# Two edits to the order of work in a two-layer image kernel: layer 1's spread of statistics and first-chunk normalisation one slice later, and the last image's loads and normalisation further ahead

## The chip, the core and the metric

The kernel runs on one NeuronCore of a Trainium2 chip. The metric is device time in microseconds: the kernel before takes 5440.93 us, the median of three runs from 5439.19 to 5442.27. The profile is of one execution with a span of 5433.7 us. The engines are named as the profile names them: PE is TensorE (matmuls), PEld its weight loads, DVE is VectorE, ACT is ScalarE, POOL is GpSimd, and SP is SyncE, which only issues DMA transfers. Each engine runs its own instructions in the order in which the built program has them, and waits on semaphores for the others.

## What is computed

The input is 16 images of 56 x 56 pixels with 384 channels, in float32. Two layers with residuals are applied. Group normalisation `_gn` takes mean and variance of an image over all pixels and 12 channels at a time (32 groups).

```python
# layer 0: dilated 3x3 attention in three groups of 128 channels (dilations 1, 2, 3), 4 heads each
x = x + proj(attention(qkv(_gn(x))))
# layer 1: depthwise 3x3 convolution with weights of sign -1, 0 or +1
x = x + depthwise(_gn(x), sign(clip(w)))
```

Each normalisation needs the statistics of a whole image before its first pixel can be normalised. So there are two barriers an image: `stats0` before layer 0, `stats1` before layer 1.

## The kernel before

An image is cut into 7 chunks of 8 rows (448 pixels), 112 chunks in all. For each chunk m three plans lay out work in slices, nine slices a chunk (`STEP = 9`):

- `plan_a` (stage A, slice 9(m - 9)): loads pixels, turns them to channels by pixels on TensorE, gathers `stats0`, stores to a DRAM scratch `xd`.
- `plan_b` (slice 9m): normalises, projects to k and v (`k_or_v`, tile `pkv`, copied out by ScalarE at L473) and q (`pq`), multiplies q and k on VectorE (`t`, L516), sums them on TensorE (`ps`), takes the softmax (`pt_s` at L536 is its first matmul, once a chunk), spreads the weights over channels (`pb_a`, L582), weighs v (`w`, L589 on VectorE and L597 on GpSimd, `y`), projects out (`po`, L615), adds the residual and gathers `stats1`, and stores to `x1d`. The edges of k and v are passed between neighbouring chunks by small DMA copies on SyncE's queue (the halos, L477 and L478).
- `plan_c` (slice 9(m + 10)): layer 1. It loads x1d in two ways. Channels 0 to 255 come as tiles `z` (in the last image `z_last`), with the rows above and below stacked on partitions, are normalised by ScalarE (and one set in four by VectorE in the last image) and convolved on TensorE (`pc`, L727, two a chunk). The last 128 channels come as `xg`, are normalised into `zg` by ScalarE (L756), multiplied tap by tap (`m`, L778) and summed on GpSimd; in the last image VectorE does the taps (L769). The result is turned back on TensorE (`pt_o`, L799), copied by ScalarE (`osb`, L801) and stored (L804): on SyncE's queue up to image 14, on ScalarE's in the last one.

The plans only call `at(when, order, piece)`: a piece is put in a list under its slice and a rank within the slice. At the end the pieces are run in sorted order, which gives the program order; the framework below then schedules instructions, engine by engine, close to that order. So a change of a slice number adds no instruction and moves instructions on several engines' queues.

The statistics of an image are a chain of six small pieces (`group_norm`), put down by `plan_b` of an image's last chunk at slices t0 + 27 + `STAT1_SLICE[k]`: aggregate by channel, mean (`pm`), deviation (`pb`), variance (`pv`), inversion on GpSimd (L345 to L349, tile `pair`), and the spreading `spread_out` on TensorE (`pp` at L354, `pz` at L367), whose results VectorE copies to `mr` and `mrz` (L358, L372). Layer 1's normalisation needs these two. In the kernel before, `spread_out` of layer 1 stands in slice t0 + 33, and the first chunk's `normalise_g` two slices later.

In the last image nothing else is left to run from the statistics on, and it takes other buffers, those of layer 0 that have become free. `z_last` takes pool `t_p` (4 buffers) for even chunks and `w_p` (3) with `xr_p` (1) for odd ones, two buffers for each of a chunk's two halves; so loads of chunk c + 2 wait for the convolutions of chunk c. For chunks 1 to 5 a half is loaded with four transfers (L702), each one with an access pattern of three shifted rows over 32 channels:

```python
three_rows = bass.AP(one.tensor, one.offset, [(W, 3), *one.ap])
nc.sync.dma_start(set_of(j, q), three_rows)
```

PSUM has three buffers (`ps_mt`) for most matmul results, `pkv`, `po`, `pt_x`, `pt_o`, `pc` and the statistics among them.

Of the kernel before, what the change touches and what calls it, by code (L numbers as in the profile page):

```python
# [35 lines left out]
def dilated_attention_then_binary_conv(  # L36
# [243 lines left out]
    def rows(ap):  # L280
        return ap.rearrange("p (r w) -> p r w", w=W)
# [6 lines left out]
    def in_one_go(matmuls):  # L288

        matmuls[0]()  # L290
        with tc.high_priority():
            for m in matmuls[1:]:
                tc.keep_in_program_order(m())
# [88 lines left out]
    def at(when, order, piece):  # L382

        pieces.setdefault((when, order), []).append(piece)
# [60 lines left out]
    def plan_b(m, t0):  # L445
# [181 lines left out]
        def norm(k):  # L627
            if k == 0:
                steps["of"] = group_norm(stats1.pop(b), lambda mr, mrz: mr1.update({b: (mr, mrz)}), True)
            steps["of"][k]()  # L630
# [20 lines left out]
        if c == NCH - 1:  # L651
            for k in range(6):
                at(t0 + 27 + STAT1_SLICE[k], STAT_ORDER[k], lambda k=k: norm(k))

    def plan_c(m, t0):

        b, c = divmod(m, NCH)
# [3 lines left out]
        def edges(j):  # L661
            found = []
            for z, _, _ in had[f"z{j}"]:
                if c == 0:
                    found.append(z[0:HD, :, 0:W])
                if c == NCH - 1:
                    found.append(z[2 * HD : 3 * HD, :, PX - W : PX])
            return found

        def set_of(j, q):  # L670
            return next(z[:, q - q0] for z, q0, q1 in had[f"z{j}"] if q0 <= q < q1)

        def load(j):
            by_set = x1d[b].rearrange("(j q c) n -> j c q n", q=NQ, c=HD)[j]
            if b < B - 1:
                z = z_p.tile([P, NQ * PX], F32, tag="z", name="z")[:K3].rearrange("p (q n) -> p q n", q=NQ)
                had[f"z{j}"] = [(z, 0, NQ)]
            else:

                had[f"z{j}"] = []  # L680
                for q0 in range(0, NQ, 2):
                    pool, tag = (t_p, "t") if c % 2 == 0 else (w_p, "w") if (j, q0) != (1, 2) else (xr_p, "xr")
                    z = pool.tile([P, 3, PX], F32, tag=tag, name="z_last")[:K3, :2]
                    had[f"z{j}"].append((z, q0, q0 + 2))
            for edge in edges(j):
                nc.gpsimd.memset(edge, 0.0)
            for ky in range(3):
                lo = W if c == 0 and ky == 0 else 0
                hi = PX - W if c == NCH - 1 and ky == 2 else PX
                n0 = p0 + (ky - 1) * W  # L690
                for z, q0, q1 in had[f"z{j}"]:
                    if b == B - 1 and 0 < c < NCH - 1:
                        continue
                    nc.sync.dma_start(
                        z[ky * HD : (ky + 1) * HD, :, lo:hi], by_set[:, q0:q1, n0 + lo : n0 + hi]
                    )
            if b == B - 1 and 0 < c < NCH - 1:

                for q in range(NQ):
                    one = by_set[:, q, p0 - W : p0 - W + PX]  # L700
                    three_rows = bass.AP(one.tensor, one.offset, [(W, 3), *one.ap])
                    nc.sync.dma_start(set_of(j, q), three_rows)  # L702

        def normalise(j):
            mrz = mr1[b][1]
            for q in range(NQ):
                z = set_of(j, q)
                if q == NQ - 1 and b == B - 1:
                    nc.vector.tensor_scalar(  # L709
                        z, z, mrz[:, j, q, 1:2], mrz[:, j, q, 0:1], op0=ALU.mult, op1=ALU.add  # L710
                    )
                    continue
                nc.scalar.activation(z, z, AF.Identity, bias=mrz[:, j, q, 0:1], scale=mrz[:, j, q, 1:2])  # L713
            for edge in edges(j):
                nc.gpsimd.memset(edge, 0.0)  # L715
# [5 lines left out]
        def convolve(j):  # L721
            pc = ps_mt.tile([P, 512], F32, tag="mt", name="pc")
            pcr = rows(pc[:, :PX])

            def tap(kx, q):
                lo, hi = max(0, 1 - kx), W - max(0, kx - 1)
                return nc.tensor.matmul(  # L727
                    pcr[q * HD : (q + 1) * HD, :, lo:hi], kdiag[:, kx, j * NQ + q, :],
                    rows(set_of(j, q))[:, :, lo + kx - 1 : hi + kx - 1], start=(kx == 1), stop=(kx == 2),
                )  # L730

            in_one_go([lambda kx=kx, q=q: tap(kx, q) for kx in (1, 0, 2) for q in (3, 0, 1, 2)])
            x1 = had["x1"]
            nc.vector.tensor_tensor(x1[:, j], pc[:, :PX], x1[:, j], ALU.add)  # L734
# [26 lines left out]
        def taps_last(ky):  # L761

            mid = had["xg"][:, 1 : ROWS + 1, :]
            if ky == 0:
                had["m"] = m_p.tile([P, 3, PX], F32, tag="m", name="m")
            acc = rows(had["m"][:, 0])
            for kx in range(3):
                o = 3 * ky + kx
                nc.vector.scalar_tensor_tensor(  # L769
                    mid if o == 8 else acc, zp[:, ky : ky + ROWS, kx : kx + W], ktap[:, o : o + 1],  # L770
                    acc if o else mid, op0=ALU.mult, op1=ALU.add,
                )

        def taps_g(ky):
            t = m_p.tile([P, 3, PX], F32, tag="m", name="m")
            for kx in range(3):
                o = 3 * ky + kx
                nc.scalar.activation(  # L778
                    rows(t[:, kx]), zp[:, ky : ky + ROWS, kx : kx + W], AF.Copy, scale=ktap[:, o : o + 1]
                )  # L780
            if ky == 0:
                had["m"] = t
            else:
                nc.gpsimd.tensor_tensor(had["m"], had["m"], t, ALU.add)  # L784
# [9 lines left out]
        def turn(s):  # L794
            pt = ps_mt.tile([P, 512], F32, tag="mt", name="pt_o")
            mid = had["xg"][:, 1 : ROWS + 1, :].rearrange("p r w -> p (r w)")
            for j in range(NG):
                src = mid if j == JG else had["x1"][:, j]
                nc.tensor.transpose(pt[:SUB, j * P : (j + 1) * P], src[:, s * SUB : (s + 1) * SUB], ident)  # L799
            osb = o_p.tile([SUB, C], F32, tag="osb", name="osb")  # L800
            nc.scalar.copy(osb, pt[:SUB, :C])  # L801

            queue = nc.sync if b < B - 1 else nc.scalar
            queue.dma_start(of[b, p0 + s * SUB : p0 + (s + 1) * SUB, :], osb)  # L804

        if b == B - 1:

            at(t0 - 6, LOADS, load_g)
            at(t0 - 3, LOADS, load_x)
            ahead = 3 if c else 1  # L810
            at(t0 - ahead, NORM, normalise_g)
            for j in range(JG):
                at(t0 - 5 + j, LOADS, lambda j=j: load(j))
                at(t0 - ahead + j, NORM, lambda j=j: normalise(j))
                at(t0 + 1 + j, CONVOLVE, lambda j=j: convolve(j))
            for ky in range(3):
                at(t0 + 1 + ky, CONVOLVE, lambda ky=ky: taps_last(ky))
            for s in range(NSUB):
                at(t0 + 12, STAGE_C, lambda s=s: turn(s))
            return  # L820
        at(t0 - 4, LOADS, load_g)
        at(t0 - 1, NORM, normalise_g)
        for ky in range(3):
            at(t0 + 2 * ky, CONVOLVE, lambda ky=ky: taps_g(ky))
        for kx in (1, 2, 3):
            at(t0 + 5 + kx, CONVOLVE, lambda kx=kx: sum_g(kx))
        at(t0 - 1, LOADS, load_x)
        for j in range(JG):
            at(t0 - 4 + 3 * j, LOADS, lambda j=j: load(j))
            at(t0 - 1 + 3 * j, NORM, lambda j=j: normalise(j))  # L830
            at(t0 + 2 + 3 * j, CONVOLVE, lambda j=j: convolve(j))
        for s in range(NSUB):
            at(t0 + 9 + s, STAGE_C, lambda s=s: turn(s))

    SOFTMAX, SCORE, STATISTICS, CONVOLVE, WEIGH, QUERY, SPREAD, QKV, PROJECT, STAGE_A, STAGE_C, NORM, LOADS = range(13)
# [1 line left out]
    STAT_ORDER = (STATISTICS, SPREAD, SPREAD, SPREAD, STATISTICS, SPREAD)  # L837
    STEP = 9
    STAT0_SLICE = (0, 1, 2, 4, 5, 7)
    STAT1_SLICE = (0, 1, 2, 4, 5, 6)  # L840
    FIRST = -200
    at(FIRST, LOADS, load_weights)
    for cc in range(NG):
# [6 lines left out]
    for m in range(N):  # L850
        plan_a(m, STEP * (m - 9))
        plan_b(m, STEP * m)
        plan_c(m, STEP * (m + 10))
# [31 lines left out]
```

## Time and profile before

| | |
|---|---|
| time, median of 3 | 5440.93 us |
| span of the profile, mean granted TensorE clock | 5433.7 us, 0.976 |
| idle TensorE of the span | 4% |
| plain chunk, period of L536 | 44.88 us |
| L727 (`pc`), matmuls of the convolution | 518.2 us over 5040 |
| last image's layer 1 statistics ready (`mr`) | 5277.9 us |
| from there to the end of the span | 155.8 us |

A row of the waits names the engine and line that stood idle, what ended its idle time, and then microseconds in total, times, and the longest. A row of a timeline has start and length in us, engine, line, tiles out and in, and in square brackets the idle time before it with its releaser. A row of windows gives length and each engine's busy time with its count of instructions, then the granted clock, the mean busy share of the 16 DMA engines, and GB/s. TensorE's float32 matmuls appear twice in counts: a group of three that the program writes is x6.

### The profile page before, as it was taken

The page shows a single profiled execution, that of the slowest core. Times are in us where ns is not written, and L with a number is a line of the kernel's source. Part 1 is how long each engine was busy: PE and PEld are TensorE (multiplying, and loading weights), DVE is VectorE, ACT ScalarE, POOL GpSimd, SP SyncE. Part 2 cuts the span into 40 slices and gives each one's busy share as a digit, 9 for nine tenths or more (in the row PEclk, how much of TensorE's full clock was granted, in tenths as well). Part 3 has the DMA queues.
Part 4 walks back from the last instruction along what each step waited for, and adds up shares of the span by engine and source line. Part 5 has one row for each costly group of instructions (what it writes and reads, how often), then busy time and mean ns, then how long its engine had stood idle before and what let it go on. Part 6 is the DMA issues. An engine that isn't in the chain of part 4 may idle for free. (4 is left out here: it accounts for less than half of the span.)

```text
span 5433.7 us, 77423 instructions
## 1 busy us (share of the span) xinstructions
PE 5223.6 (96%) x27669; PEld 2426.0 (45%) x27669; DVE 4147.1 (76%) x4209; ACT 2408.1 (44%) x4189; POOL 4212.9 (78%) x3049
## 2 busy tenths in 40 slices
PE   8999999999999999999999999999999999999965
PEld 4444444444444444444444444444444444444421
DVE  4887877878777787777878777787877877777853
ACT  3223444444444444444444444444444444444432
POOL 2677888878788887888888788888878888888860
PEclk9999999999999999999999999999999999999976
DMA  5444555655555555555655555565565656544443
GB/s 167 126 119 113 157 153 161 164 153 162 156 160 159 164 158 161 156 154 160 164 154 160 161 155 158 163 161 159 158 162 159 165 148 164 153 132 134 131 115 121
DMA packets 810799, 825.73 MB, mean 152 GB/s; under 512 B 359467, under 2 KB 800174, under 8 KB 810414
## 3 DMA queue, kind: packets, MB, share of 16 engines
q1 hardware_dynamic: 802430, 808.79, 54.2%
q10 hardware_dynamic: 7984, 12.00, 0.7%
q8 instruction: 219, 3.59, 0.3%
q14 instruction: 166, 1.36, 0.1%
HBM read 466.41 MB, written 231.21 MB: 128 GB/s over the span
## 5 line engine op out<-in xcount | busy, mean ns | idle before, releaser
L597 POOL TENSOR_TENSOR w<-w 128x1344 f32<-128x1344 f32 x672 | 2051.5, 3053 | 465.9 <-DVE w L589 403.2
L589 DVE TENSOR_TENSOR w<-pb_a,v 128x1344 f32<-128x1344 f32 x1008 | 1559.8, 1547 | 244.5 <-PE pb_a L582 167.2
L516 DVE TENSOR_TENSOR t<-pq,k 128x1344 f32<-128x1344 f32 x1008 | 1536.4, 1550 | 247.0 <-PE pq L463 247.0
L463 PE MATMUL pkv<-xn,wqkvT 128*128 128x448 f32 x3924 | 1595.1, 555 | 0.0
L463 PEld LDWEIGHTS pkv<-xn,wqkvT 128*128 128x128 f32 x3924 | 725.0, 192 | 666.6 <-issue 639.8
L615 PE MATMUL po<-y,wprojT 128*128 128x448 f32 x2016 | 827.7, 548 | 18.0 <-POOL y L601 15.1
L784 POOL TENSOR_TENSOR m<-m 128x1344 f32<-128x1344 f32 x210 | 640.7, 3051 | 260.4 <-ACT m L778 260.4
L463 PE MATMUL pq<-xn,wqkvT 128*128 128x448 f32 x1962 | 826.7, 557 | 0.0
L713 ACT ACTIVATE z<-z,mrz 96x448 f32<-96x448 f32 x840 | 580.0, 752 | 423.7 <-DMA z<-x1d 403.4
L778 ACT ACTIVATE m<-zg,ktap 128x448 f32<-128x448 f32 x945 | 552.2, 657 | 275.1 <-POOL m L784 270.5
L501 PE MATMUL ps<-t,sel 128*32 128x448 f32 x6048 | 661.6, 547 | 9.4 <-DVE t L516 8.8
L615 PEld LDWEIGHTS po<-y,wprojT 128*128 128x128 f32 x2016 | 376.8, 191 | 377.0 <-issue 348.6
L727 PE MATMUL pc<-z,kdiag 96*32 96x440 f32 (+1 forms) x5040 | 518.2, 544 | 6.9 <-POOL z L715 4.6
L463 PEld LDWEIGHTS pq<-xn,wqkvT 128*128 128x128 f32 x1962 | 345.2, 189 | 311.5 <-issue 311.5
L734 DVE TENSOR_TENSOR x<-pc,x 128x448 f32<-128x448 f32 x224 | 139.8, 624 | 419.0 <-PE pc L727 417.0
L601 POOL TENSOR_TENSOR y<-y,w 128x448 f32<-128x448 f32 x336 | 381.7, 1136 | 22.6
L600 POOL TENSOR_TENSOR y<-w 128x448 f32<-128x448 f32 x336 | 382.4, 1138 | 12.5
L582 PE MATMUL pb_a<-aT,spread 24*128 24x448 bf16 x3024 | 368.9, 359 | 23.3 <-DVE w L589 18.0
L618 DVE SCALAR_TENSOR_TENSOR xr<-po,bias,xr 128x448 f32<-128x448 f32 x336 | 227.6, 678 | 189.1 <-PE po L615 185.3
L473 ACT COPY v<-pkv 128x448 f32<-128x448 f32 x336 | 179.1, 533 | 415.3 <-PE pkv L463 398.8
L473 ACT COPY k<-pkv 128x448 f32<-128x448 f32 x336 | 178.7, 532 | 373.5 <-PE pkv L463 373.5
L424 ACT COPY xa<-pt_x 128x448 f32<-128x448 f32 x315 | 168.2, 534 | 377.6 <-PE pt_x L412 375.7
(131 smaller groups left out, 4408.5 us busy)
## 6 DMA issues: line engine op xcount, KB each, us to landing
z<-x1d SPq DMA_DIRECT2D x570, 224.0 KB
xr<-xd SPq DMA_DIRECT2D x112, 672.0 KB
x1d<-xr SPq DMA_DIRECT2D x112, 672.0 KB
xn<-xd SPq DMA_DIRECT2D x109, 672.0 KB
xin<-in_x_dram SPq DMA_DIRECT2D x108, 672.0 KB
xd<-xa SPq DMA_DIRECT2D x315, 224.0 KB
out_dram<-osb SPq DMA_DIRECT2D x420, 168.0 KB
x<-x1d SPq DMA_DIRECT2D x112, 448.0 KB
```

The costliest lines, as they stand in the source:

```text
L463: nc.tensor.matmul(dst[:, :PX], wqkvT[:, cc, o0 : o0 + P], had["xn"][:, cc, :], start=(cc == 0), stop=(cc == NG - 1))
L501: return nc.tensor.matmul(had["ps"][32 * j : 32 * j + 32, :PX], sel[:, s0 : s0 + 32], tk, start=(issued[j] == 1), stop=(issued[j] == len(r ...
L516: nc.vector.tensor_tensor(t.rearrange("p k (r w) -> p k r w", w=W), q3, k3, ALU.mult)
L589: nc.vector.tensor_tensor(w.rearrange("p k (r w) -> p k r w", w=W), pb[:, :, :PX].rearrange("p k (r w) -> p k r w", w=W), three(kv[1][g][m ...
L597: nc.gpsimd.tensor_tensor(w0, w0, w, ALU.add)
L600: nc.gpsimd.tensor_tensor(y, w0[:, 0], w0[:, 1], ALU.add)
L601: nc.gpsimd.tensor_tensor(y, y, w0[:, 2], ALU.add)
L615: nc.tensor.matmul(po[:, :PX], wprojT[:, g, j * P : (j + 1) * P], had[f"y{g}"], start=(g == 0), stop=(g == NG - 1))
L713: nc.scalar.activation(z, z, AF.Identity, bias=mrz[:, j, q, 0:1], scale=mrz[:, j, q, 1:2])
L727: return nc.tensor.matmul(pcr[q * HD : (q + 1) * HD, :, lo:hi], kdiag[:, kx, j * NQ + q, :], rows(set_of(j, q))[:, :, lo + kx - 1 : hi + k ...
L778: nc.scalar.activation(rows(t[:, kx]), zp[:, ky : ky + ROWS, kx : kx + W], AF.Copy, scale=ktap[:, o : o + 1])
L784: nc.gpsimd.tensor_tensor(had["m"], had["m"], t, ALU.add)
```

## The change

Two things move, and no instruction is added or taken away.

For images 0 to 14, `spread_out` of layer 1 goes from slice t0 + 33 to t0 + 34 (the last entry of `STAT1_SLICE`, which holds for the last image too), and what the first chunk (c == 0) does with it, `normalise_g`, the taps, `normalise` and `convolve`, goes one slice on as well (`late`). The aim is to give the chain on GpSimd, which inverts the deviation, more time before TensorE comes to the spreading.

For the last image, the loads of a chunk's `xg` and `z_last` go from 6 and 5 slices ahead of the chunk to 12, and its normalisation from 3 to 8 (chunk 0 stays at 1). The aim is to have the transfers of the end begin earlier.

```diff
         if b == B - 1:
-            at(t0 - 6, LOADS, load_g)
+            at(t0 - 12, LOADS, load_g)
             at(t0 - 3, LOADS, load_x)
-            ahead = 3 if c else 1
+            ahead = 8 if c else 1
             at(t0 - ahead, NORM, normalise_g)
             for j in range(JG):
-                at(t0 - 5 + j, LOADS, lambda j=j: load(j))
+                at(t0 - 12 + j, LOADS, lambda j=j: load(j))
                 at(t0 - ahead + j, NORM, lambda j=j: normalise(j))
...
+        late = 1 if c == 0 else 0
         at(t0 - 4, LOADS, load_g)
-        at(t0 - 1, NORM, normalise_g)
+        at(t0 - 1 + late, NORM, normalise_g)
         for ky in range(3):
-            at(t0 + 2 * ky, CONVOLVE, lambda ky=ky: taps_g(ky))
+            at(t0 + 2 * ky + late, CONVOLVE, lambda ky=ky: taps_g(ky))
...
-            at(t0 - 1 + 3 * j, NORM, lambda j=j: normalise(j))
-            at(t0 + 2 + 3 * j, CONVOLVE, lambda j=j: convolve(j))
+            at(t0 - 1 + 3 * j + late, NORM, lambda j=j: normalise(j))
+            at(t0 + 2 + 3 * j + late, CONVOLVE, lambda j=j: convolve(j))
...
-    STAT1_SLICE = (0, 1, 2, 4, 5, 6)
+    STAT1_SLICE = (0, 1, 2, 4, 5, 7)
```

## The prediction

> **What bounds the kernel now.** I read the page's busy times and slices first, then the waits of TensorE, then the timeline of one image boundary, then the chain and the timelines of the last 160 us.
>
> ```profile
> PE 5223.6 (96%) x27669; PEld 2426.0 (45%) x27669; DVE 4147.1 (76%) x4209; ACT 2408.1 (44%) x4189; POOL 4212.9 (78%) x3049
> PE   8999999999999999999999999999999999999965
> PEclk9999999999999999999999999999999999999976
> ```
>
> TensorE is the bound except in the last two slices, where its share and its clock drop. Its idle time is 5433.7 - 5223.6 = 210 us. The waits of TensorE (total, count, longest) are headed by these two, of which the first lies in the tail:
>
> ```profile
> PE pc L727 <- DVE z_last L709: 47.9, 9, 8.3
> PE pp L354 <- POOL pair L349: 44.8, 16, 5.2
> ```
>
> The second is the matmul that spreads the group statistics to channels, waiting for GpSimd's inverse deviation. The timeline of TensorE shows one case (start, us, what, idle before):
>
> ```profile
> 1750.22 0.36 PE L582 MATMUL pb_a<-aT,spread 24*128 24x448 bf16 x3
> 1753.18 0.82 PE L354 MATMUL pp<-pair,gselT 32*128 32x2 f32 x6 [2.60 <-POOL pair L349]
> 1753.94 0.68 PE L367 MATMUL pz<-pair,gselT 32*32 32x2 f32 x48
> 1754.54 3.85 PE L463 MATMUL pkv<-xn,wqkvT 128*128 128x448 f32 x6
> ```
>
> It waits 2.60 us, and the six key/value matmuls behind it take 3.85 us where half of a usual group of twelve (4.78 us) is 2.39. The windows after the stall and 40 us earlier show why: the column ahead of the DMA share is the granted clock.
>
> ```profile
> 1754.50:1758.40 3.90, 3.90 (x21) 1.45 (x12) 1.64 (x2) 0.55 (x1) 1.96 (x1) 0.64 0.06 16
> 1712.00:1714.00 2.00, 2.00 (x10) 0.77 (x12) 1.97 (x3) 0.67 (x2) 2.00 (x2) 1.00 0.07 13
> ```
>
> So a stall costs its length and then some microseconds at a lower clock. All of it together is read from the period of the once-a-chunk softmax transpose L536, whose starts are
>
> ```profile
> 1676.24 1.04 PE L536 MATMUL pt_s<-perm,sT 128*112 128x128 f32 x8
> 1721.12 1.04 PE L536 MATMUL pt_s<-perm,sT 128*112 128x128 f32 x8
> 1773.15 1.04 PE L536 MATMUL pt_s<-perm,sT 128*112 128x128 f32 x8
> ```
>
> A plain chunk is 44.88 us, the chunk with layer 1's statistics 52.03. All 14 such chunks between 750 and 5020 us sum to 732.9 us.
>
> The tail: the chain of waits is made of loads of z_last and little else, and the issues on SyncE's queue (start, us, count) show the stream.
>
> ```profile
> 5286.77 0.34 SPq L804 DMA_DIRECT2D out_dram<-osb  x1
> 5287.17 7.39 SPq L702 DMA_DIRECT2D z_last<-x1d  x6
> ...
> 5300.00 16.92 SPq L702 DMA_DIRECT2D z_last<-x1d  x8
> ...
> 5321.53 17.70 SPq L702 DMA_DIRECT2D z_last<-x1d  x8
> ...
> 5342.66 21.61 SPq L702 DMA_DIRECT2D z_last<-x1d  x9
> ```
>
> Eight loads a chunk at 16.92 / 8 = 2.1 us or 17.70 / 8 = 2.2 us, 21 us from chunk to chunk, with one pause (5389 to 5393) up to the last load's issue at about 5407; the end follows some 26 us later. In the window from 5312 to 5316, with only these loads in flight, 76 GB/s move at a DMA share of 0.20.
>
> [...] 0.64 of the clock after the 2.60 us stall, 1.00 elsewhere[...]. [...] ScalarE ran nothing between 1744.2 and 1754.2 while its zg activation (L756) waited 10.01 us for the statistics. [...]
>
> **The change part by part.**
>
> *Spreading one slice on (STAT1 6 to 7).* In the built order of the changed kernel's TensorE instructions, two key/value groups (x12 in the trace's count), one of the output projection (x6) and one more pb_a now stand between the weighing group pb_a and pp. By the trace's rows that is 4.78 + 2.42 + 0.36, about 7.5 us of ready work. GpSimd's chain, whose order there is the same, needs 2.60 us (3.23 at most, 5.16 in the first image). The wait goes, and with it the low clock. Worth: the statistics' own matmuls, start to start, are pm 0.28, pb 0.75, pv 0.28, pp 0.76, pz 0.60, sum 2.67 us; a boundary without a stall should take 44.88 + 2.67 = 47.55 us. So 732.9 - 14 x 47.55 = 67 us for 14 boundaries. The first, at 442 us, had 5.16 us of wait and then 4.38 us for six pkv matmuls instead of 2.39, 1.44 instead of 0.82 for pp and 1.02 instead of 0.68 for pz: 8 us. Sum 75.
>
> *First chunk's normalisation, taps and convolution one slice on (late).* It adds no instruction; it follows the spreading so that ScalarE doesn't wait at zg. Queued behind zg on ScalarE was the copy of v (L473), for which PSUM's next key/value group waits; in the new order v and k stand ahead of zg. What is later: ScalarE's taps and pc of chunk 0, by some 5 us. pc's reader is the output turn, six slices on, so that is hidden. The z loads of chunk 1 need chunk 0's buffer, and stand in SyncE's queue ahead of halo copies of k and v: they would wait some 1 us longer. The copy of k now stands behind three taps that wait for GpSimd's m (up to 2.7 us in the trace, in other chunks, where it costs TensorE nothing). Bounds: nothing to 1 us a boundary; I take 0.3 us, 5 us in all. Boundaries: -70 us.
>
> *Last image, loads 12 ahead.* In the trace chunk 1's L702 loads are issued one at 5282 and the rest from 5287 to 5298, because an output (L804) of the image before stands ahead of them, and its copy stands on ScalarE behind the zg that waits for the statistics (mr at 5277.9). In the new order all eight stand ahead of that output, from about 5261 with buffers free since 5252, so they land by about 5283 while chunk 0 still computes. Chunk 2's loads need chunk 0's convolutions, which ended at 5285.7 and 5292.1: the stream, which began chunk 2 at 5300.0, can begin it at 5286. From there on nothing gets faster: the same 2.2 us a load on three engines. The end moves by 14 to 17 us; I take 15. Bounds: 0 (outputs or buffers block it again) and 20.
>
> *Last image, normalisation 8 ahead.* It puts ScalarE's z_last work ahead of output copies of the chunk before. ScalarE and VectorE are idle more than half the tail (30.0 and 31.8 us busy of 108 from 5301 to 5409), and the loads come last anyway: nothing by itself.
>
> *The spreading one slice on, in the last image:* pc still stands ahead of pp, as before: nothing.
>
> Sum: 5440.9 - 70 - 15 = 5356 us.
>
> **The rivals.** (1) Both parts pay: 5356. (2) The boundaries pay, the tail doesn't, because the three-engine stream holds it whatever its start or an output copy blocks the queue again: 5440.9 - 70 = 5371. For it: SyncE's queue is in order and six outputs still stand among the loads. Against: the first eight loads need nothing that is late. (3) Half of each boundary returns as a wait on ScalarE's copies or on halo loads: 5440.9 - 35 - 15 = 5391. For it: the k copy behind the taps. Against: the copy lagged its matmuls by 3 us in other chunks with no stall. (4) Slower: the later z loads hold the k and v halos, and TensorE stands for a whole slice (44.88 / 9 = 5.0 us) with 3 us of low clock after, against 75 / 15 = 5.0 us saved: 15 x 3.0 = +45, tail -15, 5471. Against: the z loads are held by about 1 us only. (5) The new waits just eat the gain: about 5440.
>
> **How the numbers follow.** Chances: (1) 0.72, (2) 0.12, (3) 0.09, (5) 0.03, (4) 0.04. Faster 0.93, same 0.03, slower 0.04. The low end takes 75 us at the boundaries, the 20 of the tail and 8 for short start-up waits that may go (two of 3 us near 480 us): 5338. The high end takes 55 at the boundaries and nothing in the tail: 5386. That leaves out most of (3), (4) and (5), and a little of (1).
>
> **What would show it.** Right: the wait of pp for pair gone from TensorE's list but for the first image's layer 0; zg's 163 us of waiting for mr on ScalarE mostly gone; the boundary period of L536 near 47.6 us; clock 1.00 across boundaries; chunk 1's L702 issued before 5281 on the old scale, chunk 2's from some 23 us after; 2.2 us a load as before. Wrong: boundary periods above 50 us, new TensorE waits for ScalarE's k or VectorE's t there, or a tail from the last statistics' mr to the end that still lasts 155 us.

## The result, and the profile after

The changed kernel takes **5408.54 us** (median of four runs, 5405.9 to 5415.36) against 5440.06 us (5436.75 to 5442.27) for the kernel before beside it: a ratio of 0.9944, 95% interval 0.9927 to 0.9962. It is faster by 31.5 us, where 85 were predicted; the time lies above the predicted range.

The page of the kernel after, TensorE's busy time and the clock by slice:

```profile
PE 5205.9 (96%) x27669; PEld 2414.4 (45%) x27669; DVE 4150.0 (77%) x4209; ACT 2397.8 (44%) x4189; POOL 4215.2 (78%) x3049
PEclk9999999999999999999999999999999999999976
```

TensorE is busy 17.7 us less than before (5223.6) with the same 27669 matmuls: that fits with less time run at a low clock (mean granted clock of the span 0.980, before 0.976). Its waits in the kernel after (total us, times, longest):

```profile
PE pb_a L582 <- DVE w L589: 25.9, 25, 4.7
PE ps L501 <- DVE t L516: 25.3, 34, 1.7
...
PE po L615 <- ACT k L473: 9.7, 10, 1.4
...
PE pp L354 <- POOL pair L349: 2.4, 1, 2.4
```

The wait that the change was aimed at has gone from 44.8 us to the one of layer 0. In its place come short waits: `ps` for VectorE's t, `pb_a` for VectorE's w, and `po` for the k copy, which was 2.9 us (4 times) before. The first two in the kernel before:

```profile
PE pb_a L582 <- DVE w L589: 18.0, 6, 4.7
...
PE ps L501 <- DVE t L516: 8.8, 13, 2.9
```

ScalarE's waits of zg show the same trade. Before:

```profile
ACT zg L756 <- DVE mr L358: 163.0, 16, 11.1
...
ACT zg L756 <- DMA xg<-x1d: 28.3, 34, 2.1
```

After:

```profile
ACT zg L756 <- DMA xg<-x1d: 114.6, 51, 8.9
...
ACT zg L756 <- DVE mr L358: 74.1, 16, 8.8
```

Where those short waits lie is seen from the starts of `pt_s`, one a chunk, at the same image boundary that the prediction showed. Timeline of TensorE after (start, us):

```profile
1706.72 1.04 PE L536 MATMUL pt_s<-perm,sT 128*112 128x128 f32 x8
1754.29 1.04 PE L536 MATMUL pt_s<-perm,sT 128*112 128x128 f32 x8
1801.30 1.04 PE L536 MATMUL pt_s<-perm,sT 128*112 128x128 f32 x8
1848.77 1.04 PE L536 MATMUL pt_s<-perm,sT 128*112 128x128 f32 x8
```

The chunk with the statistics takes 47.57 us instead of 52.03, as worked out in the prediction. But the next two take 47.01 and 47.47, where the kernel before has 44.89 and 45.71 (it starts them at 1773.15, 1818.04 and 1863.75). Three chunks together gain 0.6 us. The same differences, as means over the same 12 images in each kernel's profile, for the kernels that bear on the boundaries (us; the times are medians of each run; where additions are left out, the output lacks those taps):

| kernel | statistics' chunk | next | 2nd | 3rd | time |
|---|---|---|---|---|---|
| before | 52.45 | 44.88 | 45.99 | 46.59 | 5440.06 |
| changed | 47.57 | 47.25 | 48.18 | 46.54 | 5408.54 |
| both boundary edits | 47.57 | 47.08 | 48.54 | 46.56 | 5427.23 |
| spreading alone | 47.57 | 50.75 | 45.90 | 46.49 | 5438.69 |
| boundary edits, no additions in chunk 0 | 47.57 | 45.54 | 48.45 | 46.37 | 5391.13 |
| boundary edits, none in chunks 0 and 1 | 47.57 | 45.53 | 45.97 | 46.56 | 5358.26 |
| before, none in chunks 0 and 1 | 52.61 | 44.88 | 45.99 | 46.57 | 5425.60 |
| boundary edits, early loads | 47.57 | 47.04 | 46.86 | 46.59 | 5418.33 |
| changed, early loads | 47.57 | 47.04 | 47.08 | 46.60 | 5403.50 |
| changed, chunk 0's additions on VectorE | 47.57 | 51.07 | 46.92 | 46.51 | 5440.59 |
| changed, tap work 4, 2, 1 slices later | 47.57 | 49.06 | 49.31 | 47.17 | 5499.77 |
| the same, early z loads | 47.57 | 47.32 | 49.37 | 49.43 | 5500.38 |

The chunk called next holds the tap work of image chunk 0, the 2nd that of image chunk 1. The remaining three chunks of an image stay within 0.1 us of 44.9, but in the last two rows. In the changed kernel the statistics' chunk gains 4.88 us, the two behind it lose 2.37 and 2.19. The first boundary, not in these means, went from 50.3 to 42.0 and the chunk behind it from 54.7 to 53.2.

What happens in the first of those chunks is read from three engines' timelines of the kernel after, between 1754 and 1779 us. GpSimd first:

```profile
1753.50 3.06 POOL L784 TENSOR_TENSOR m<-m 128x1344 f32<-128x1344 f32 x1 [2.33 <-ACT m L778]
...
1758.94 3.05 POOL L597 TENSOR_TENSOR w<-w 128x1344 f32<-128x1344 f32 x1 [2.18 <-DVE w L589]
1761.96 3.42 POOL L784 TENSOR_TENSOR m<-m 128x1344 f32<-128x1344 f32 x1
1765.45 2.35 POOL L789 TENSOR_TENSOR m<-m 128x448 f32<-128x448 f32 x2
1767.77 1.16 POOL L559 TENSOR_TENSOR rest<-ew,e 112x512 f32<-112x512 f32 x1
```

The tap additions of image chunk 0 (L784, L789) are still being worked off, without a gap, when the softmax's `rest` is due; it starts 13.5 us after `pt_s`. In the kernel before, the same additions begin 7 us ahead of `pt_s` (1773.15), and `rest` starts 9.1 us after it, having waited for ScalarE and not for GpSimd's queue:

```profile
1766.23 3.06 POOL L784 TENSOR_TENSOR m<-m 128x1344 f32<-128x1344 f32 x1
...
1771.25 3.04 POOL L784 TENSOR_TENSOR m<-m 128x1344 f32<-128x1344 f32 x1 [1.74 <-ACT m L778]
1774.37 2.35 POOL L789 TENSOR_TENSOR m<-m 128x448 f32<-128x448 f32 x2
...
1782.21 1.17 POOL L559 TENSOR_TENSOR rest<-ew,e 112x512 f32<-112x512 f32 x1 [1.25 <-ACT e L558]
```

Behind `rest`, in the kernel after, on ScalarE, VectorE and TensorE:

```profile
1768.96 0.62 ACT L563 CAST e<-rest 112x512 bf16<-112x512 f32 x1 [5.42 <-POOL rest L559]
```

```profile
1770.05 0.63 DVE L425 BATCH_NORM_STATS2 stats<-xa 128x6 f32<-128x448 f32 x1 [1.87 <-ACT xa L424]
...
1774.16 1.56 DVE L589 TENSOR_TENSOR w<-pb_a,v 128x1344 f32<-128x1344 f32 x1 [1.50 <-POOL w L597]
```

```profile
1775.77 0.37 PE L582 MATMUL pb_a<-aT,spread 24*128 24x448 bf16 x3 [0.60 <-DVE w L589]
...
1777.24 1.71 PE L501 MATMUL ps<-t,sel 128*32 128x448 f32 x16 [0.57 <-DVE t L516]
```

ScalarE stands 5.42 us at a cast and has the copy of xa behind it; VectorE stands for that copy and then for a free w buffer, which GpSimd's next w addition has to release; TensorE stands for VectorE. No single wait of TensorE in this chunk is over a microsecond. It is idle for 1.39 us of the 47.01; the other 0.7 us of the excess is busy time at a clock of 1.00 (45.62 us against 44.89 in the kernel before, for the same work), and what makes that longer isn't known.

The tail came out nearly as predicted. SyncE's queue after (start, us, count), the last image's statistics reaching `mr` at 5268.35:

```profile
5257.82 0.85 SPq L702 DMA_DIRECT2D z_last<-x1d  x1
5259.21 1.55 SPq L702 DMA_DIRECT2D z_last<-x1d  x2
5261.44 8.88 SPq L702 DMA_DIRECT2D z_last<-x1d  x5
5276.22 2.25 SPq L702 DMA_DIRECT2D z_last<-x1d  x3
...
5328.77 21.09 SPq L702 DMA_DIRECT2D z_last<-x1d  x9
```

Chunk 1's eight loads are issued from 5257.82 to 5270.3, nearly all of them before `mr` exists; chunk 2's begin at 5276.22, which is 5285.8 on the old scale (9.6 us added, by which `mr` came earlier); the rate is unchanged (21.09 / 9 = 2.3 us a load). From `mr` to the end are 136.9 us instead of 155.8.

### The profile page after: what moved, and what is told of

It is laid out like the page before. It is cut to its first block, busy times and chain, and to the rows that moved or that the text cites. A ratio compares the mean times of both kernels' runs of the same rounds, so it can differ in the third digit from the quotient of the medians.

```text
span 5405.2 us, 77297 instructions
## 1 busy us (share of the span) xinstructions
PE 5205.9 (96%) x27669; PEld 2414.4 (45%) x27669; DVE 4150.0 (77%) x4209; ACT 2397.8 (44%) x4189; POOL 4215.2 (78%) x3049
## 5 line engine op out<-in xcount | busy, mean ns | idle before, releaser
L463 PE MATMUL pkv<-xn,wqkvT 128*128 128x448 f32 x3924 | 1569.9, 549 | 9.0 <-ACT xa L424 4.7
L784 POOL TENSOR_TENSOR m<-m 128x1344 f32<-128x1344 f32 x210 | 644.7, 3070 | 274.1 <-ACT m L778 274.0
L501 PEld LDWEIGHTS ps<-t,sel 128*32 128x32 f32 x6048 | 170.6, 110 | 364.9 <-issue 247.8
```

Source lines behind the costliest of these rows:

```text
L463: nc.tensor.matmul(dst[:, :PX], wqkvT[:, cc, o0 : o0 + P], had["xn"][:, cc, :], start=(cc == 0), stop=(cc == NG - 1))
L501: return nc.tensor.matmul(had["ps"][32 * j : 32 * j + 32, :PX], sel[:, s0 : s0 + 32], tk, start=(issued[j] == 1), stop=(issued[j] == len(r ...
```

## The experiments

Theories, once the result was known: the gain at the boundaries is given back in the next two chunks, either through GpSimd's queue, which no longer gets the 5 us in which TensorE stood (A), or through loads that come late on SyncE's queue (B), or through `late` itself.

**1. The tail alone** (in the kernel before).

```
-            at(t0 - 6, LOADS, load_g)
+            at(t0 - 12, LOADS, load_g)
...
-            ahead = 3 if c else 1
+            ahead = 8 if c else 1
...
-                at(t0 - 5 + j, LOADS, lambda j=j: load(j))
+                at(t0 - 12 + j, LOADS, lambda j=j: load(j))
```

> The last image's part alone: loads 12 slices ahead, normalisation 8; boundaries as before. Working theory: the two parts are independent, and the tail's gain is what the trace of the changed kernel shows from the start of the last plain chunk on, 28.5 us in all less 9.5 before it, so 19 us: about 5421 us, with boundary periods of 52 to 54 us as before. Rival (the tail profits only because the boundaries brought the work closer together): less than 10 us, above 5430.

Measured: 5424.76 us, ratio 0.9972 (0.9962 to 0.9982): 14.6 us faster, less than the 19 expected here, and what the prediction gave for the tail (15).

**2. The boundary edits alone** (the changed kernel, with the last image's slices as before).

```
-            at(t0 - 12, LOADS, load_g)
+            at(t0 - 6, LOADS, load_g)
...
-            ahead = 8 if c else 1
+            ahead = 3 if c else 1
...
-                at(t0 - 12 + j, LOADS, lambda j=j: load(j))
+                at(t0 - 5 + j, LOADS, lambda j=j: load(j))
```

> The boundary part alone: spreading one slice on and the first chunk's work late, last image as before. Working theory: the 4.5 us saved at a boundary is given back in the next two chunks (periods 47.0 where 44.9 stood, and 1 to 4 us more in the one after), so only the first boundary's 8 us and 1 to 2 us more are left: about 5430 us. Rival (the early loads of the last image disturb the rest): 5380 or lower with the next chunk at 44.9.

Measured: 5427.23 us, ratio 0.9975 (0.9966 to 0.9985): 12.1 us where 70 were predicted. The miss is here; the two parts alone make 26.7 us, which lies within the interval of the 31.5 measured together (0.9927 to 0.9962 is 40 to 21 us). The periods add up to it: 14 x (-4.88 + 2.20 + 2.55) = -1.8, the first boundary -8.3 and its next chunk -1.5 make -11.6.

**3. The spreading alone** (as run 2, without `late`: the kernel before with the last entry of `STAT1_SLICE` 7).

> Only the spreading one slice on (STAT1 7); the first chunk's normalisation, taps and convolution stay in their slices, which are still behind it. If late is what gives the gain back (taps and convolution crowding the chunk after), the next chunk's period falls from 47.0 to about 44.9 and the time goes to about 5370. If the crowding comes from TensorE no longer standing still, so that GpSimd's tap sums and softmax's rest meet in any case, the period stays at 46 to 48 and the time near 5430.

Measured: 5438.69 us, ratio 0.9997 (0.9989 to 1.0006). Without `late` the loss in the next chunk is larger (50.75), and the one behind it loses nothing (45.90). So `late` moves part of the loss into the second chunk, and on balance it doesn't cost but saves 11.5 us.

**4. Chunk 0's tap additions on GpSimd left out** (images 0 to 14; the output lacks those taps), with both boundary edits.

```
+                if c == 0 and b < B - 1:
+                    return
                 nc.gpsimd.tensor_tensor(had["m"], had["m"], t, ALU.add)
```

and the same ahead of the addition in `sum_g` for kx < 3.

> The boundary part alone, with the tap sums of the first chunk of images 0 to 14 left out on GpSimd (two additions of 3 x 448 and two of 448, 8.4 us); the products on ScalarE stay. Theory of GpSimd's queue: softmax's rest stands behind these sums, ScalarE stands 5.4 us at the cast that needs rest, the copy of xa behind it is late, VectorE waits for it in order, and TensorE waits for VectorE. Then without the sums ScalarE's wait at the cast falls to about 1.3 us, the next chunk's period to 44.9 to 45.2, and the time to about 5370. Rival (SyncE's queue, where z loads now stand among the halo copies, or ScalarE's own order): period stays at 47.0 and the time near 5430.

Measured: 5391.13 us, ratio 0.9911 (0.9897 to 0.9924). The next chunk falls from 47.08 to 45.54, most of its excess, but the one behind it stays at 48.45. In the whole run `po` still waits for the k copy, 17.6 us in 14 times. This left A and B open for that second chunk.

**5. The same for chunks 0 and 1** (`if c <= 1`).

> Both boundary edits, no edit of the tail; the tap additions on GpSimd of the first AND the second chunk of images 0 to 14 are left out (so the output lacks those taps). With the first chunk's left out alone the kernel took 5391.13 us, and its periods of L536 were 47.6 (statistics), 45.5, 48.4, 46.4. The disputed 48.4 (46.0 in the kernel before) is that of the second chunk after the statistics. Theory A, GpSimd's own backlog (the second chunk's additions are still late, so VectorE's first product finds no free w buffer and the operations behind it, and the k copy that stands behind the tap products, are late too): 48.4 falls to 46.0 to 46.5, 15 x about 2.2 = 33 us less, 5358. Theory B, late loads (the halo and xg loads stand behind the transposed aT load on SyncE's queue): the loads are no earlier, 48.4 stays and the time is 5385 to 5391.

Measured: 5358.26 us, ratio 0.9849 (0.9836 to 0.9863), what theory A gave. Timeline of TensorE in this run:

```profile
1690.61 1.04 PE L536 MATMUL pt_s<-perm,sT 128*112 128x128 f32 x8
1738.18 1.04 PE L536 MATMUL pt_s<-perm,sT 128*112 128x128 f32 x8
1783.71 1.04 PE L536 MATMUL pt_s<-perm,sT 128*112 128x128 f32 x8
1829.43 1.04 PE L536 MATMUL pt_s<-perm,sT 128*112 128x128 f32 x8
```

47.57, 45.53 and 45.72 us: with these additions gone, about 0.65 us of give-back is left, all in the next chunk. The loads, untouched in code, also come back to their old place: the first z load behind the weights' transposed load is issued 16.1 us after `pt_s` in the second chunk, as in the kernel before, against 18.4 with the boundary edits alone (means of 12).

**6. The control: the same omission in the kernel before.**

> The kernel before (5439.4 us), with nothing of the change, and the tap additions on GpSimd of the first two chunks of images 0 to 14 left out (so the output lacks those taps). With both boundary edits the same omission gave 5358.26 instead of 5427.23 us, 69 us. If those additions cost time only because the statistic chunk no longer waits 2.6 us and so leaves GpSimd behind: the period of the statistic chunk stays at 52.4, those of the next two go from 44.9 and 46.0 to 44.9 and 45.9, only the first image's second chunk gains (54.7 to about 46.5), and the time is 5430. If leaving GpSimd work out helps whatever the boundary does: 69 us here too, 5370.

Measured: 5425.60 us, ratio 0.9970 (0.9959 to 0.9982), 15 us. Outside the first image the periods are those of the kernel before, and the targeted wait is as it was:

```profile
PE pp L354 <- POOL pair L349: 44.9, 16, 5.2
```

The chunk behind the first image's boundary gained more than expected (54.7 to 43.7). The same GpSimd work therefore costs 69 us in the kernel with the boundary edits and 15 in the one without. Read the other way: with these additions the boundary edits bring 12.1 us, without them 67 (5425.60 to 5358.26), close to the 70 predicted. While TensorE lost 4.9 us at each boundary, GpSimd's additions had time; without that loss they are what TensorE waits for, through the other engines. Which link carries how much (`rest`, the w buffers, the m buffers for which ScalarE's tap products wait) these runs don't separate.

**7. Early loads**, with both boundary edits: xg and z two slices earlier, ahead of the weights' transposed load on SyncE's queue.

```
-        at(t0 - 4, LOADS, load_g)
+        at(t0 - 6, LOADS, load_g)
...
-            at(t0 - 4 + 3 * j, LOADS, lambda j=j: load(j))
+            at(t0 - 6 + 3 * j, LOADS, lambda j=j: load(j))
```

> Both boundary edits, no edit of the tail (5427.23 us), and for every image but the last the loads of xg and of both z groups two slices earlier, ahead of the transposed aT load on SyncE's queue. Theory B (late loads): zg's 115 us of waiting for xg falls under 30, the period of the second chunk after the statistics falls from 48.5 to about 46.2, that of the first from 47.1 to 46.5: 14 x 2.9 = 40 us less, 5387. Theory A (GpSimd's backlog): zg's wait goes as well, but the periods stay within 0.3 us and the time lies between 5421 and 5431.

Measured: 5418.33 us, ratio 0.9960 (0.9947 to 0.9972). Neither expectation holds whole. ScalarE's wait for z falls from 334.2 to 164.7 us and the next chunk stays at 47.04, so late z loads are no cause there. zg's wait for xg stays at 103.5 us (114.7 before this edit), so this run doesn't test late xg; in run 5 that wait is as long (99.7 us), and the next chunk takes 45.53. In the second chunk 1.7 of the excess 2.5 us go (48.54 to 46.86), with these waits on TensorE:

```profile
PE ps L501 <- DVE t L516: 13.6, 24, 1.7
...
PE po L615 <- ACT k L473: 10.8, 13, 1.6
```

(28.8 and 14.8 us with the boundary edits alone). Together with run 5: the late z loads are a link of the second chunk's chain, and GpSimd's lateness is what makes them late, since the transposed load that stands ahead of them waits for its `e` (L564; SyncE's waits for it are 143.6 us in 22 times in the changed kernel, 55.8 in 9 in the kernel before). The second chunks of the twelve images gain 20 us by this, the time only 8.9: image 14's chunks and the stretch behind the last `pt_s` (243.0 us became 250.6) lose some 13 us, and why isn't known.

**8. Early loads in the changed kernel.**

> The changed kernel (5408.54 us) with the loads of xg and z of every image but the last two slices earlier. With the boundary edits alone these loads brought 5427.23 to 5418.33, 8.9 us, all of it in the second chunk after the statistics (48.55 to 46.87). If that adds to the tail's gain: 5399.6. If the tail's stream of loads collides with it: 5405 or more.

Measured: 5403.50 us (5398.18 to 5407.27), ratio 0.9935 (0.9921 to 0.9948). That lies between the two expectations. It is the fastest kernel here that computes everything; its advantage of 5 us over the changed kernel comes from ratios whose intervals overlap.

**9. Chunk 0's L784 on VectorE, in the changed kernel.**

```
-                nc.gpsimd.tensor_tensor(had["m"], had["m"], t, ALU.add)
+                eng = nc.vector if c == 0 else nc.gpsimd
+                eng.tensor_tensor(had["m"], had["m"], t, ALU.add)
```

> The changed kernel (5408.54 us) with the first chunk's two 3x448 tap additions of each image (L784, 3.05 us each on GpSimd) on VectorE. Theory A with VectorE free enough: GpSimd loses 6.1 of its 266 us an image just where it is late, the period of the next chunk falls from 47.2 to about 45.7, 14 x 1.5 = 21 us less, 5388. Rival: [...] (L549 took 1.27 us instead of 0.65 in the chunk where GpSimd ran late), so that each costs VectorE 3 us or more in front of the products that TensorE waits for: no gain or a loss, 5408 to 5425.

Measured: 5440.59 us, ratio 1.000 (0.9991 to 1.0008): the whole gain of the change is lost, more than the rival allowed. The additions by engine in this run (minimum/median/maximum ns; line 785 here is line 784 of the others):

```profile
L785 POOL TENSOR_TENSOR m<-m x180: 3011/3047/3090, 489.0 to 5279.8; 128x1344 f32<-128x1344 f32 x180
...
L785 DVE TENSOR_TENSOR m<-m x30: 1550/3642/4969, 464.9 to 5053.2; 128x1344 f32<-128x1344 f32 x30
```

At its shortest VectorE needs 1.55 us for an addition that takes GpSimd 3.05; its median is 3.64 and its worst 4.97, in front of the products that TensorE waits for (`pb_a` for w: 66.6 us in 35 times). One of the long ones, and what GpSimd ran beside it:

```profile
1774.77 4.97 DVE L785 TENSOR_TENSOR m<-m 128x1344 f32<-128x1344 f32 x1
```

```profile
1775.29 3.04 POOL L597 TENSOR_TENSOR w<-w 128x1344 f32<-128x1344 f32 x1
1778.28 2.48 POOL L564 TENSOR_TENSOR e<-rest,e 112x512 bf16<-112x512 f32 x1
```

VectorE's addition ends 1.4 us after GpSimd's w addition, about its own length, and GpSimd's next, 1.16 us in the kernel after, ends 1.0 us behind that. In the one that took 1.55 us (at 5043.91) it is GpSimd's operation that is long: its w addition of 5043.62 takes 4.76 us. In both cases one of two additions that overlap is long: 4.97 us against 1.55 at its shortest, and 4.76 against 3.05 of a usual one. Why isn't shown.

**10. Tap products, additions and output transposes of chunks 0, 1 and 2 later by 4, 2 and 1 slices, in the changed kernel.**

```
+        lag = {0: 4, 1: 2, 2: 1}.get(c, 0)
...
-            at(t0 + 2 * ky + late, CONVOLVE, lambda ky=ky: taps_g(ky))
+            at(t0 + 2 * ky + max(late, lag), CONVOLVE, lambda ky=ky: taps_g(ky))
...
-            at(t0 + 5 + kx, CONVOLVE, lambda kx=kx: sum_g(kx))
+            at(t0 + 5 + kx + lag, CONVOLVE, lambda kx=kx: sum_g(kx))
...
-            at(t0 + 9 + s, STAGE_C, lambda s=s: turn(s))
+            at(min(t0 + 9 + s + lag, t0 + 13 + s // 2) if lag else t0 + 9 + s, STAGE_C, lambda s=s: turn(s))
```

> The changed kernel with the tap products, the tap additions and the output transposes of the first three chunks of an image 4, 2 and 1 slices later (images 0 to 14): the same work, so placed that GpSimd's queue has the additions behind the products of attention and not ahead of them. If GpSimd's order at the boundary is the cause of what the next two chunks give back (47.2 and 48.2): about 45.5 and 46.5, 14 x 3.4 = 48 us less, 5361. If GpSimd is short of capacity and not of order there (266 us busy of 323 an image): the loss only moves to the chunks behind, 5400 to 5415.

Measured: 5499.77 us, ratio 1.0112 (1.0096 to 1.0128), a miss of both. The waits of TensorE in this run:

```profile
PE ps L501 <- DVE t L516: 48.2, 39, 1.9
PE pb_a L582 <- DVE w L589: 44.1, 41, 5.3
PE po L615 <- ACT v L473: 23.2, 16, 3.7
```

Putting the work behind others doesn't make it harmless: the waits for VectorE have grown, and there is now also one for ScalarE's v copies. I haven't taken this chain apart further, so whether another order of the same additions would keep the gain stays open.

**11. The same with the z loads two slices earlier** (run 7's second edit).

> As the run with the lags of 4, 2 and 1, and the loads of both z groups two slices earlier for images 0 to 14 (xg stays, since its buffer is still in use). If late halo loads are what is left of the second chunk's loss: 3 to 10 us under the run with the lags alone; if the lag has already taken the loss away: within 3 us of it.

Measured: 5500.38 us, ratio 1.0117 (1.0102 to 1.0132): within 3 us of run 10. The earlier z loads don't change the time there.

**12. The last image's loads alone ahead, its normalisation and the boundaries as before** (in the kernel before):

```
-            at(t0 - 6, LOADS, load_g)
+            at(t0 - 12, LOADS, load_g)
...
-                at(t0 - 5 + j, LOADS, lambda j=j: load(j))
+                at(t0 - 12 + j, LOADS, lambda j=j: load(j))
```

> The kernel before (5439.4 us) with only the last image's loads twelve slices ahead; its normalisation stays where it was. With loads and normalisation both ahead the gain was 14.7 us. If the earlier start of the stream of loads is the whole gain: 5425. If the loads need the earlier normalisation to free their buffers in time: within 4 us of 5439.

Measured: 5422.14 us, ratio 0.9967 (0.9954 to 0.9979), 17 us. The loads alone bring the tail's gain; the normalisation ahead adds nothing that these runs show.

## Why the prediction was wrong

- **Spreading one slice on.** Right in mechanism and size, for the chunk it looked at: the wait of `pp` is gone, the clock shows 1.00 there (1743 to 1747 us), the period is 47.57 against 47.55 worked out, and the first boundary gained 8.3 us for the 8 said.
- **The step that failed** is the one that turned this into a sum: "Bounds: nothing to 1 us a boundary; I take 0.3 us, 5 us in all." It priced only what `late` delays, and took everything else behind the stall as waiting for TensorE alone. Measured (run 2), a boundary gives back 2.20 and 2.55 us in the two chunks behind it, 4.75 us and not 0.3; times 14 that is 66 us, against 5. Runs 5 and 6 show the cause: GpSimd's tap additions of chunks 0 and 1, which fall right behind the statistics and had been covered by the stall. Without them the boundary edits bring 67 us.
- **The bounds were too narrow** for the same reason. Row 1 of the page showed GpSimd at 78%, but over one image of the kernel before it was 266.0 of 325.1 us, 82%, and the taps of chunk 0 can't be worked ahead of the statistics, since zg waits for `mr`. The prediction named the k copy behind the taps only as a risk of `late`. Rival (3), half of each boundary returning, was nearest in kind at 0.09, but looked for it on ScalarE and in the halo loads; these are later links of the chain. Nearly all of a boundary returned, not half; that is what rival (5) says, "The new waits just eat the gain", given 0.03, though it didn't see that the first boundary and the tail would keep theirs.
- **`late`.** It was priced at 5 us of cost; on balance it saves 11.5 us (run 2 against run 3).
- **The tail.** 15 us predicted, 14.6 measured alone, in the way named: stream earlier, same rate (2.3 us a load, 2.1 to 2.4 before); the normalisation ahead adds nothing visible (run 12). That the stream ran on three engines is an estimate from the DMA share before, 0.20 x 16 = 3.2. In the profiles of the changed kernel and the one before it is 18.9.
- **What would show it.** The signs for "right" came true but for one: zg's wait for `mr` was to be mostly gone and fell only from 163.0 to 74.1 us. A sign for "wrong" came true too, more TensorE waits for k and t. The list had no period of the chunks behind the boundary, where the loss lay.
- **Two readings.** The clock was 1.00 around the plain chunks but not everywhere "elsewhere": from 5301 to 5409 us, in the tail of the kernel before, it was 0.66. And the tail's groups of loads start 21.5, 21.1 and 24.9 us apart, not evenly 21. Neither bears on the miss.

One link may lie between VectorE and GpSimd themselves. In the second chunk of the kernel after, VectorE's L549 overlaps with a w addition of GpSimd:

```profile
1809.79 1.27 DVE L549 TENSOR_TENSOR ew<-ew,sm 112x432 f32<-112x432 f32 x1
```

```profile
1807.53 3.06 POOL L597 TENSOR_TENSOR w<-w 128x1344 f32<-128x1344 f32 x1
```

It ends at 1811.06, 0.47 us after GpSimd's addition. On average it takes 1.27 us in that chunk after the change, 0.65 before, and 0.59 in run 5. In run 9, too, an addition of VectorE took longer beside one of GpSimd (4.97 us, 1.55 at its shortest). It may be one cause of the later transposed load; no run takes it away by itself.

## What to carry to other kernels

When a stall is taken from the bounding engine, look up which other engine was catching up during it: measure its work in the stretch right behind the stall, not its share over the span, and give the change no more than that engine's slack there. Judge such an edit by the periods of the chunks behind the one it improves, since a gain can be returned in many waits of half a microsecond. Before moving work from GpSimd to VectorE, look at what GpSimd runs beside it, and price the operation as it runs there: in run 9 that was a median of 3.64 us, not the 1.55 of its shortest.

## What the runs showed that I had not expected

- An addition of 128x1344 that takes VectorE 1.55 us at its shortest took a median of 3.64 us beside GpSimd's work, longer than GpSimd's own 3.05; and where VectorE's took 1.55 us, GpSimd's w addition beside it took 4.76.
- Two waits of TensorE of 0.60 and 0.57 us within 4 us (1775 to 1779 us in the kernel after, 2.83 us busy in 4.00) left the clock at 1.00. In the kernel before, the boundary stalls of images 1 to 14, of 2.6 to 3.2 us, were each followed by 3.9 us at a mean clock between 0.50 and 0.64.
- The order of the tap work is worth more than its amount suggests: 4, 2 and 1 slices of lag on the same instructions cost 91 us.
